# Pair attention kernel: the six pair adds that GpSimd makes per block, written in six other forms

## The chip, the cores and the metric

The kernel runs on one core of one Trainium2 chip. Its metric is the device time of one execution in microseconds (us), of which lower is better. A core has a TensorE for matmuls (PE in the profile, its weight loads PEld), a VectorE (DVE), a ScalarE (ACT), a GpSimd (POOL) and a SyncE (SP) that issues most DMAs. Each engine works through its own instructions in the order of the program, and waits on semaphores where it needs another engine's result.

## The reference

The reference is a network of two layers on an input of 4 sequences of 1024 tokens with 256 channels. Each layer has a layer norm with a modulation, an attention part, another modulated layer norm and a feed-forward part. Layer 0 is a recurrence over time followed by a mixture of eight experts. Layer 1, which the change belongs to, is a pair attention followed by a dense feed-forward net of hidden width 1024 (w1, w2, h1, h2, w3). Cut to what matters, its attention is:

```
q = einsum('bnc,ac->bna', X, Wq)          # 64 channels a
k = einsum('bnc,ac->bna', X, Wk)
Vy = einsum('bnc,dc->bnd', X, Wy_w) + Wy_b
e = relu(rho(q[:, :, None, :] + k[:, None, :, :]))
scores = einsum('bija,a->bij', e, Wphi)
ex = exp(scores - max(scores, axis=-1))
denom = sum(ex, axis=-1)
part1 = einsum('bij,bjc->bic', ex, Vy)
Ew = einsum('bij,bija->bia', ex, e)
part2 = einsum('bia,ca->bic', Ew, We_w) + We_b * denom
out = (part1 + part2) / (denom + 1e-9)
```

Here rho(x) is sqrt(relu(x) + 1e-8) - sqrt(relu(-x) + 1e-8). For every query i, key j and channel a the sum q + k is formed, clipped at zero, and its root taken. These are 4 x 1024 x 1024 x 64 values, and they set the work of this layer.

## The kernel before, in words

The first part of the kernel (to about 1088 us in the profile) computes layer 0 and the keys, queries and values of the first sequence. The rest is the function `pair_attention`, which computes the pair attention of layer 1, with its feed-forward net and the remainder of layer 0 woven in.

`pair_attention` works on N = 128 blocks of 32 queries each, 32 blocks for each of the 4 sequences. A block (class `Block`) has 16 tiles of 128 partitions x 1024 keys. A tile's partitions are 8 channels by 16 queries; its number i (0 to 15) says which of 8 channel groups and which half of the queries it holds. Two tiles make a pair p (0 to 7; i = 2p + h), which lies in one buffer of the ring "s" of RING = 14 buffers of 128 x 2 x 1024 floats. A buffer passes through these steps:

- The add: relu(key + query), where the keys kB[i % 8] are a 128 x 1024 tile in SBUF and the query is one number per partition, `self.query(i)`. Which engine makes it depends on i. In all blocks but the first, the six tiles of ADD_ON_POOL = (1, 3, 5, 9, 11, 13) are made by GpSimd in `begin` (line 1396), the five of RELU_ON_SCALAR = (2, 6, 8, 12, 14) by ScalarE in `pair` (line 1418), and the other five (0, 4, 7, 10, 15) by VectorE in `adds` (line 1407). The first block has none on GpSimd, so that GpSimd makes 127 x 6 = 762 adds.
- The root: ScalarE takes the square root of the whole pair in place (line 1419, 128 x 2048).
- The scores: TensorE multiplies the roots by the weights of their channels and adds them up in the block's PSUM tile "sc" (line 1423, 16 matmuls for a pair).
- When the block's 8 pairs are in, `top` (line 1433), `exps` (line 1442) and `spread` (line 1449) take the largest score, the exponentials, and spread these over the partitions into the PSUM tile "xb".
- `weigh` (line 1469): VectorE multiplies each of the 16 tiles by xb in place and sums along the keys into a column of "ew". After the second tile of a pair its ring buffer is free again.

The order on each engine is the order in which the Python code issues the instructions. The loop at the end of `pair_attention` goes over the blocks and over p. At each step it issues `weigh` for pair p of the present block and `adds` for the pair that is next to be finished, then (at p = 5 and 6) `top`, `exps` and `spread` of the next block, then a share of other work (`work`, which draws on the generators `finish` and `dense`), and then `begin` and `make` up to 14 pairs ahead. `begin` for a pair runs LEAD = 2 pairs ahead of `make`, which issues the rest of the add, the root and the scores. So GpSimd's adds run 2 pairs ahead of the root that needs them, and up to 14 pairs ahead of the `weigh` that frees their buffer.

`finish` ends four blocks at a time: it multiplies by values and weights, divides, and GpSimd adds the result to the residual (line 1544, "xr"). `dense` is the feed-forward net for 256 tokens (lines 1260 to 1362), whose last step is also an add on GpSimd (line 1362, "res"). In layer 0 GpSimd makes the products "kv" (line 745), products "rk" (line 437), the sums "xi" (line 414) and others, all of them tensor-by-tensor instructions.

Of the kernel before, what the change touches and what calls it, by code (L numbers as in the profile page):

```python
# [9 lines left out]
ALU = mybir.AluOpType  # L10
# [4 lines left out]
P = 128  # L15
B, T, C = 4, 1024, 256
# [19 lines left out]
FIRST_ON_SCALAR = 6  # L36
ADD_ON_POOL = (1, 3, 5, 9, 11, 13)
LEAD = 2

CONSTS = {"ident": P, "tri": P, "ones": P, "avg": P, "center": P, "heads": P, "gather": P, "rank": NE, "same": P, "pick": 4 * P, "part": 4, "query": 16, "row0": P}  # L40
CH_MX, CH_MW, CH_MK, CH_MV, CH_MR, CH_MG, CH_TD, CH_U, CH_LW, CH_LB = range(10)
# [3 lines left out]
def block_kernel(ctx: ExitStack, tc: tile.TileContext, a, out):  # L45
# [26 lines left out]
    nc.gpsimd.memset(seen, 0.0)  # L72
    first_layer(tc, a, link, cols, seen, ident, eps)
    pair_attention(tc, a, link, out, cols, seen, ident, eps)


# [762 lines left out]
def pair_attention(tc, a, link, out, cols_of, seen, ident, eps):  # L839
# [10 lines left out]
    nc = tc.nc  # L850
# [4 lines left out]
    with tc.tile_pool(name="at_k", bufs=1) as pk, tc.tile_pool(name="at_w", bufs=1) as wp, tc.tile_pool(  # L855
# [14 lines left out]
        kB, qtab, kds, vds = {0: {}}, {0: link["qt"][0]}, {0: link["kd"]}, {0: link["vd"]}  # L870
# [17 lines left out]
        for i in range(2):  # L888
            t = wp.tile([P, 4, P], F32, tag=f"ewt{i}", name=f"ewt{i}")
            nc.gpsimd.memset(t, 0.0)  # L890
            ewt.append(t)
            t = wp.tile([P, 4, 64], F32, tag=f"ew{i}", name=f"ew{i}")
# [485 lines left out]
        class Block:  # L1378
# [9 lines left out]
            def query(self, i):  # L1388
                return qtab[self.b][:, 2 * (self.n % NB) + i // 8, i % 8 : i % 8 + 1]

            def begin(self, p):
                self.s[p] = ring.tile([P, 2, T], F32, tag="s", name="s")
                for h in range(2):
                    i = 2 * p + h
                    if self.n and i in ADD_ON_POOL:
                        nc.gpsimd.tensor_scalar(  # L1396
                            self.s[p][:, h, :], kB[self.b][i % 8], self.query(i), 0.0, ALU.add, ALU.max
                        )

            def adds(self, p):  # L1400
                if p in self.added:
# [190 lines left out]

        for _ in range(LEAD):
            begin()
        for _ in range(8):
            begin()
            make()
# [3 lines left out]
        while begun < ahead[0]:  # L1601
            begin()
            make()
# [134 lines left out]
```

## Time and profile before

| What | Value |
|---|---|
| Two runs | 4984.17 us and 4977.72 us, median 4980.94 us |
| Span of the profiled execution, first to last instruction | 4972.7 us |
| GpSimd's adds of line 1396 | 762, from 1088.9 us to 4789.1 us, 2879.2 us busy |
| VectorE's adds of line 1407 | 645, 595.3 us busy |
| ScalarE's relus of line 1418 | 641, 728.9 us busy |
| ScalarE's roots of line 1419 | 1024, 2028.2 us busy |
| VectorE's weighing, line 1469 | 2048, 2419.0 us busy |

The record of the profiled execution has its span and no time of its own. The median of the two runs is 4980.94 - 4972.7 = 8.2 us above that span. A row of the profile's groups gives the line, the engine, the operation, output and inputs by the program's names, shapes and count, and after the bar the busy time in us, the mean duration of one in ns, the time that the engine sat idle just before these instructions, and what ended most of this idle time. Busy shares of several engines add up to more than the span, since they work side by side.

### The profile page before, as it was taken

How to read it: one execution, taken by the hardware profiler on the slowest of the kernel's cores; microseconds unless marked ns; L12 is line 12 of the kernel's file. 1: busy time of each engine (PE TensorE's matmuls, PEld its weight loads, DVE VectorE, ACT ScalarE, POOL GpSimd, SP SyncE). 2: the span in 40 equal slices, each digit the busy share in tenths (PEclk: the TensorE clock that was granted, in tenths of full speed). 3: DMA queues.
4: the chain of work that ended last, by engine and by line, in shares of the span. 5: the costliest groups of instructions: out<-in, count | busy, mean ns of one | idle time of the engine just before them, and what ended most of it. 6: DMA issues, size and time to landing. Idle time of an engine off the chain costs nothing.

```text
span 4972.7 us, 75609 instructions
## 1 busy us (share of the span) xinstructions
PE 4289.7 (86%) x28714; PEld 2423.9 (49%) x28714; DVE 4175.6 (84%) x7255; ACT 3688.3 (74%) x3436; POOL 3397.2 (68%) x1231
## 2 busy tenths in 40 slices
PE   6899999886879788988887988889798889888888
PEld 1233333332346455545554655545455555455557
DVE  5899999868998888898887888888888888888871
ACT  2333333238898898899998998999888989999961
POOL 3544444336887787888786887887777878887840
PEclk8799999887999899989997999999899999999999
DMA  4333333440022222312112332212132322112223
GB/s 139 94 117 116 108 110 111 131 141 19 23 65 85 74 90 68 125 56 79 64 62 81 108 108 83 71 58 86 48 119 75 110 70 86 60 69 76 73 83 113
DMA packets 255947, 429.42 MB, mean 86 GB/s; under 512 B 71784, under 2 KB 142624, under 8 KB 255328
## 3 DMA queue, kind: packets, MB, share of 16 engines
q1 hardware_dynamic: 252512, 422.09, 26.2%
q8 instruction: 227, 3.72, 0.3%
q10 hardware_dynamic: 2880, 1.98, 0.1%
q14 instruction: 136, 1.11, 0.1%
q0 software_dynamic: 192, 0.52, 0.0%
HBM read 400.32 MB, written 40.93 MB: 89 GB/s over the span
## 4 chain that ended last, share of the span: by engine, by line
PE 50%; DVE 20%; ACT 20%; issue 7%; DMA 1%; SPq 1%; POOL 1%; DVEq 0%; ACTq 0%; POOLq 0%
PE ff_ps L1330 14%; PE sc L1423 10%; ACT s L1419 9%; DVE s L1469 9%; PE e_ps L620 7%; ACT s L1418 4%; DVE s L1407 3%; PE xb L1449 3%; PE out_ps L1351 2%; PE o L1520 2%; PE proj_ps L425 2%; ACT L1419 2%; DVE state L813 1%; PE mix_ps L405 1%; ACT L1372 1%
## 5 line engine op out<-in xcount | busy, mean ns | idle before, releaser
L1396 POOL TENSOR_SCALAR s<-kB,qt 128x1024 f32<-128x1024 f32 x762 | 2879.2, 3792 | 603.5 <-DVE ew L1469 476.2
L1469 DVE CUSTOM_DVE_ANT_0 s<-s,xb 128x1024 f32<-128x1024 f32 x2048 | 2419.0, 1211 | 38.4 <-PE xb L1449 36.8
L1419 ACT ACTIVATE s<-s,eps 128x2048 f32<-128x2048 f32 x1024 | 2028.2, 2000 | 84.0 <-DVE s L1407 38.5
L1423 PE MATMUL sc<-s,wsel 128*32 128x256 f32 x16384 | 1199.1, 417 | 399.4 <-ACT s L1419 397.0
L1330 PE MATMUL ff_ps<-wide,fw 128*128 128x256 f32 x4096 | 1005.3, 395 | 29.4 <-ACT wide L1372 25.8
L1423 PEld LDWEIGHTS sc<-s,wsel 128*32 128x32 f32 x16384 | 456.8, 116 | 1002.7 <-ACT s L1419 593.6
L1330 PEld LDWEIGHTS ff_ps<-wide,fw 128*128 128x128 f32 x4096 | 765.4, 194 | 237.5 <-issue 99.4
L1418 ACT ACTIVATE s<-kB,qt 128x1024 f32<-128x1024 f32 x641 | 728.9, 1137 | 18.7 <-DVE acc L603 18.0
L1407 DVE TENSOR_SCALAR s<-kB,qt 128x1024 f32<-128x1024 f32 x645 | 595.3, 924 | 0.3 <-issue 0.3
L745 POOL TENSOR_TENSOR kv<-vb,out_k 128x512 f32<-128x512 f32 x256 | 324.5, 1276 | 236.9 <-DVE state L813 157.3
L620 PE MATMUL e_ps<-wd,hid 128*128 128x512 f32 x896 | 414.7, 609 | 7.4 <-DVE acc L603 4.8
L1449 PE MATMUL xb<-ex,pick 64*128 64x256 f32 x2048 | 324.3, 440 | 56.2 <-ACT ex L1442 56.2
L813 DVE TENSOR_TENSOR_SCAN state<-dec,carry,kv 128x512 f32<-128x512 f32 x256 | 326.1, 1274 | 22.6 <-ACT dec L800 16.8
L1449 PEld LDWEIGHTS xb<-ex,pick 64*128 64x128 f32 x2048 | 195.4, 206 | 193.8 <-ACT ex L1442 96.1
L620 PEld LDWEIGHTS e_ps<-wd,hid 128*128 128x128 f32 x896 | 169.9, 195 | 231.3 <-issue 217.4
L1260 PE MATMUL ff_ps<-wide,fw 128*128 128x256 f32 x1024 | 266.2, 409 | 6.1 <-ACT wide L944 5.8
L805 ACT COPY carry<-state 128x1 f32<-128x1 f32 x255 | 47.9, 188 | 297.9 <-DVE state L813 297.5
L1260 PEld LDWEIGHTS ff_ps<-wide,fw 128*128 128x128 f32 x1024 | 197.6, 202 | 64.8 <-issue 25.6
L1314 DVE TENSOR_TENSOR wide<-ff_ps,ffn_s 128x512 f32<-128x512 f32 x128 | 87.9, 687 | 166.9 <-PE ff_ps L1330 166.9
L1433 DVE TENSOR_REDUCE sc<-sc 128x1 f32<-128x256 f32 x128 | 54.9, 429 | 204.5 <-PE sc L1423 204.3
L1442 ACT ACTIVATE ex<-sc,neg 128x256 f32<-128x256 f32 x128 | 60.7, 474 | 199.1 <-DVE neg L1440 198.3
L815 DVE TENSOR_TENSOR pr<-state,rec 128x512 f32<-128x512 f32 x256 | 176.0, 688 | 37.8 <-ACT state L811 10.5
(253 smaller groups left out, 3965.8 us busy)
## 6 DMA issues: line engine op xcount, KB each, us to landing
fw<-in_ffw_dram SPq DMA_DIRECT2D x354, 512.0 KB
vb<-vd SPq DMA_DIRECT2D x1024, 64.0 KB
lent<-vd SPq DMA_DIRECT2D x64, 514.0 KB
wd<-in_w_down_dram SPq DMA_DIRECT2D x28, 1024.0 KB
kB<-kd SPq DMA_DIRECT2D x32, 512.0 KB
lent<-in_We_dram SPq DMA_DIRECT2D x32, 512.0 KB
kd<-nd SPq DMA_DIRECT2D x24, 512.0 KB
vd<-out_v SPq DMA_DIRECT2D x8, 512.0 KB
```

The source lines that it names most:

```text
L620: nc.tensor.matmul(ps, hid[:, k, t * P : (t + 1) * P], wd[:, k, :], start=k == 0, stop=k == HID // P - 1)
L745: nc.gpsimd.tensor_mul(kv, vb[:, g % 2, :], ready[u]["k"][:, n // HN, :])
L813: nc.vector.tensor_tensor_scan(s[:, 1 : U + 1], dec, kv, c, ALU.mult, ALU.add)
L1260: nc.tensor.matmul(ps[:, h, :], w[:, k, o : o + P], hT[:, k, :], start=k == 0, stop=k == 1)
L1330: nc.tensor.matmul(ps[:, h, :], w[:, k * P : (k + 1) * P], of[:, k, :], start=k == 0, stop=k == 7)
L1396: nc.gpsimd.tensor_scalar(self.s[p][:, h, :], kB[self.b][i % 8], self.query(i), 0.0, ALU.add, ALU.max)
L1407: nc.vector.tensor_scalar(self.s[p][:, h, :], kB[self.b][i % 8], self.query(i), 0.0, ALU.add, ALU.max)
L1418: nc.scalar.activation(t[:, h, :], kB[self.b][i % 8], AF.Relu, bias=self.query(i))
L1419: nc.scalar.activation(t, t, AF.Sqrt, bias=eps_rho)
L1423: nc.tensor.matmul(self.sc[32 * j : 32 * j + 32, 0:256], wsel[:, g, 16 * (1 - s) : 16 * (1 - s) + 32], t[:, h, 256 * j : 256 * (j + 1)], s ...
L1449: nc.tensor.matmul(xb[:, 256 * j : 256 * (j + 1)], pick[q, j % 2, s, :], self.ex[q, :], start=True, stop=True)
L1469: nc.vector.tensor_tensor_reduce(t[:, h, :], t[:, h, :], self.xb[s], 1.0, 0.0, ALU.mult, ALU.add, ew[:, self.n % 4, col : col + 1])
```

## The change

`begin` no longer issues one `tensor_scalar` with add and max for each of the six tiles. It calls a new method, `pool_add`, which writes each tile number in its own form. Tile 13 keeps the one instruction. The other five have two instructions each, the second of which works in place on the tile t that the first has written. All instructions go over 128 x 1024 floats.

| Tile | First instruction | Second instruction, in place |
|---|---|---|
| 13 | (k + query) max 0 | none |
| 3 | (k * 1) + query | (t min FLT_MAX) max 0 |
| 5 | (k + query) * 1 | t max 0 |
| 9 | tensor by tensor: k + query, the query's column read 1024 times | (t max 0) min FLT_MAX |
| 11 | k + query | (t max 0) + 0 |
| 1 | (k * 1) + query | (t max 0) * 1 |

The result is the same in each form. In all there are 11 instructions per block in place of 6, that is 127 x 11 = 1397 in place of 762.

```diff
+FLT_MAX = 3.4028234e38
...
+            def pool_add(self, i, t, k):
+                q = self.query(i)
+                if i == 13:
+                    nc.gpsimd.tensor_scalar(t, k, q, 0.0, ALU.add, ALU.max)
+                elif i == 3:
+                    nc.gpsimd.tensor_scalar(t, k, 1.0, q, ALU.mult, ALU.add)
+                    nc.gpsimd.tensor_scalar(t, t, FLT_MAX, 0.0, ALU.min, ALU.max)
+                elif i == 5:
+                    nc.gpsimd.tensor_scalar(t, k, q, 1.0, ALU.add, ALU.mult)
+                    nc.gpsimd.tensor_scalar_max(t, t, 0.0)
+                elif i == 9:
+                    nc.gpsimd.tensor_tensor(t, k, q.to_broadcast([P, T]), ALU.add)
+                    nc.gpsimd.tensor_scalar(t, t, 0.0, FLT_MAX, ALU.max, ALU.min)
+                elif i == 11:
+                    nc.gpsimd.tensor_scalar_add(t, k, q)
+                    nc.gpsimd.tensor_scalar(t, t, 0.0, 0.0, ALU.max, ALU.add)
+                else:
+                    nc.gpsimd.tensor_scalar(t, k, 1.0, q, ALU.mult, ALU.add)
+                    nc.gpsimd.tensor_scalar(t, t, 0.0, 1.0, ALU.max, ALU.mult)
+
             def begin(self, p):
                 self.s[p] = ring.tile([P, 2, T], F32, tag="s", name="s")
                 for h in range(2):
                     i = 2 * p + h
                     if self.n and i in ADD_ON_POOL:
-                        nc.gpsimd.tensor_scalar(
-                            self.s[p][:, h, :], kB[self.b][i % 8], self.query(i), 0.0, ALU.add, ALU.max
-                        )
+                        self.pool_add(i, self.s[p][:, h, :], kB[self.b][i % 8])
```

## The prediction

> **What bounds the kernel now.** I read the page's busy shares first, then the chain of work that ended last, then the groups; after these the answer for GpSimd's add line, the groups of GpSimd alone, and the busy times by window.
>
> ```profile
> span 4972.7 us, 75609 instructions
> ...
> PE 4289.7 (86%) x28714; PEld 2423.9 (49%) x28714; DVE 4175.6 (84%) x7255; ACT 3688.3 (74%) x3436; POOL 3397.2 (68%) x1231
> ...
> PE 50%; DVE 20%; ACT 20%; issue 7%; DMA 1%; SPq 1%; POOL 1%; DVEq 0%; ACTq 0%; POOLq 0%
> ...
> L1396 POOL TENSOR_SCALAR s<-kB,qt 128x1024 f32<-128x1024 f32 x762 | 2879.2, 3792 | 603.5 <-DVE ew L1469 476.2
> ```
>
> No engine fills the span, and the chain passes from TensorE to VectorE to ScalarE; GpSimd has 1% of it. By the pair stage alone, from 1300 to 4785 us, the engines stand much closer:
>
> ```profile
> 1300.00:4785.00 3485.00, 3008.21 (x24135) 1836.53 (x24136) 3050.34 (x5427) 3157.26 (x2367) 2773.91 (x776) 0.91 0.23 78
> ```
>
> The columns are the stretch, its length, then the busy time of PE, PEld, DVE, ACT and POOL, the granted clock (0.91), the DMA share and GB/s. ScalarE is busy for 91%, VectorE for 88%, TensorE for 86%, GpSimd for 80%. So GpSimd is off the path but only 711 us of 3485 away from filling the stage. The next question is who waits for whom at its adds.
>
> ```profile
> L1396 POOL TENSOR_SCALAR s<-kB,qt x762: 3689/3700/4664, 1088.9 to 4785.0; 128x1024 f32<-128x1024 f32 x191
> its engine sat idle before it (us, times) until:
>   DVE ew L1469: 476.2, 207
> ...
> who waited for it (us, times):
>   POOL xr L1544: 21.1, 11
>   ACT s L1419: 1.2, 1
>   PEld sc L1423: 0.2, 1
> ```
>
> GpSimd waits for VectorE's weighing to free a ring buffer; almost nobody waits for GpSimd. A cheaper add on GpSimd is therefore worth next to nothing by this route, while a dearer one costs nothing until the slack is used up, and from there all of it.
>
> **The price of the forms.** The only `tensor_scalar` of GpSimd in this trace is add with max: 3.70 us at the median and 3.79 in the mean. Back to back it is the same: these are three in 11.05 us, 3.68 each, after 1.87 us of idle time.
>
> ```profile
> 3003.42 11.05 POOL L1396 TENSOR_SCALAR s<-kB,qt 128x1024 f32<-128x1024 f32 x3 [1.87 <-DVE ew L1469]
> ```
>
> The other rows of GpSimd that help:
>
> ```profile
> L745 POOL TENSOR_TENSOR kv<-vb,out_k 128x512 f32<-128x512 f32 x256 | 324.5, 1276 | 236.9 <-DVE state L813 157.3 <-DMA vb<-vd 74.7 <-DMA wd<-in_w_down_dram 3.0
> L437 POOL TENSOR_TENSOR rk<-out_r,out_k 128x1024 f32<-128x1024 f32 x8 | 18.8, 2348 | 0.8 <-ACT out_r L430 0.8
> L890 POOL MEMSET ewt<- 128x512 f32 x2 | 1.0, 524 | 13.0 <-PE yp L776 13.0
> L893 POOL MEMSET ew<- 128x256 f32 x2 | 0.6, 311 | 0.0
> ```
>
> A memset grows by (524 - 311) / 256 = 0.83 ns per element, so 1024 elements would take 0.95 us, 0.10 of it fixed. A product of two tensors of 128x1024 takes 2.35 us. One tensor with two operations takes 3.70 us, more than two tensors with one operation: the cost of a `tensor_scalar` here is not in reading, it is in the operations.
>
> - Tile 13 keeps its instruction, 3.79 us.
> - Seven new instructions have two operations in other pairs (tiles 3 and 1 both of theirs, tile 5 its first, tiles 9 and 11 their second). Bounds: 0.95 us (memset) and 4.66 us (the longest add with max). The nearest row by far is the same instruction on the same shape, and I take its 3.79: 7 x 3.79 = 26.53 us.
> - Two have one operation (tile 5's max, tile 11's add). Bounds: 0.95 and 3.79 us. If the two operations of the known row share 3.70 - 0.10 = 3.60 us evenly, one takes 1.80 + 0.10 = 1.90 us, and with the 0.09 by which the known row's mean lies above its median 1.99. I take this, since it lies below the 2.35 of one operation that has to read two tensors: 2 x 1.99 = 3.98 us.
> - Tile 9's add of two operands: 2.35 us from the product's row. That its second operand repeats one column is shown nowhere; bounds 0.95 and 3.79.
> - The in-place second instruction follows its first on the same engine. Any wait between the two is bounded by 0 and by the 0.30 us that GpSimd's DMA of line 610 sat idle after the sum of line 608 that it sends, at most 5 x 0.30 = 1.5 us per block; I take 0, as the adds in the row above run back to back.
>
> Per block: 3.79 + 26.53 + 3.98 + 2.35 = 36.65 us, against 6 x 3.79 = 22.75 before.
>
> **From GpSimd's block to the time.** When GpSimd is the bound, the time is what stands before its first add, its queue, and what follows its last. Its first add starts at 1088.9 us. Its other instructions up to its last add take 47 us (148.4 busy from 1088.9 to 1300 and 2773.9 to 4785, less the adds). Of the 63 us that it sits idle in the first 211 us, where the rest of layer 0 is still running, I keep about half, 30. From the end of its last add at 4789.1 to the end of the span there are 184 us, in which two blocks are weighed and the last feed-forward group runs; that part is on other engines and keeps its length. Sum: 1089 + 47 + 30 + 184 = 1350, plus 127 blocks. With 22.75 us this floor is 1350 + 2889 = 4239, well under 4972.7; it reaches the span at (4972.7 - 1350) / 127 = 28.5 us per block, where the ten new instructions would have (28.5 - 3.79) / 10 = 2.47 us each. With 36.65 it is 1350 + 4655 = 6005 us. The median lies 8 us above the profiled span, so the forecast is 6013, rounded to **6010 us**.
>
> Behind GpSimd's late tile stands ScalarE's root of that pair (line 1419); behind this on ScalarE's queue are the next relus, the exponentials and the feed-forward activations, and TensorE's scores wait for the root. The ring does not take up the delay: 14 buffers hold 6 pairs more than a block, which smooths one late block, not 127. Nor do the residual adds (lines 1544 and 1362) on GpSimd's queue gain new waits: their inputs come from steps some 14 pairs older than the adds ahead of them.
>
> VectorE's own adds (line 1407) run beside GpSimd's: 739 ns at the least, 751 at the median, 924 in the mean, 2137 at the most. More instructions on GpSimd may stretch them. Bounds: all of the excess over the least goes, 645 x 0.185 = 119 us less, or each costs the most, 645 x 1.213 = 782 us more. In the forecast VectorE has at least 1000 us of idle time more than now, which covers either; I take 0.
>
> **Two rules against the rows.** The Trainium skill's page "GPSIMD Engine Reference", section 4.1 Engine selection, says of GpSimd's elementwise work that "1-input is roughly line-rate", which by its clock and width would be about 0.85 us for 1024 elements. The row of add with max, one input, says 3.70. By the rule the block would have 3.79 + 9 x 0.85 + 2.35 = 13.8 us and the change would be free, at 4981; I keep to the row. The page "SBUF — State Buffer", section Who interferes with whom, says that VectorE in a 2-port mode and GpSimd block each other for a whole instruction. VectorE's adds, 0.75 us at the median beside GpSimd's 3.70, do not show waits of that length.
>
> **The rivals.**
>
> - The forms are cheap and nothing changes (4980 us). The mechanism is a special path on GpSimd for other pairs of operations than add with max; it decides from a mean of 2.47 us for the ten new instructions. For it speaks the memset at 0.83 ns per element, which shows that the engine can go through elements four times as fast as in the add; against it that the only `tensor_scalar` seen goes at 3.6. Chance 0.20.
> - The same, and VectorE's adds also get their 119 us back with nearly all of it on the path: 4981 - 119 = 4862 us, 2.4% less. VectorE has but 20% of the chain. Chance 0.04.
> - Only max and min are dear. Then the three pairs of times and plus and the single add take 1.99 us, and the four pairs with max or min, the single max and tile 13 take 3.79: 6 x 3.79 + 4 x 1.99 + 2.35 = 33.05 us, 1350 + 4197 + 8 = 5555 us. Nothing in the profile parts the price of add from that of max. With it goes the case that the forms are cheap but VectorE's adds pay for it: 782 us less its 435 us of idle time in the stage, about 5330. Chance for 5080 to 5740 together 0.20.
> - One operation costs as much as two: 10 x 3.79 + 2.35 = 40.25 us, 1350 + 5112 + 8 = 6470 us, and with 0.30 us of wait for each second instruction 6660. Chance for over 6270: 0.18.
>
> **How the numbers follow.** The forecast's own case, 34.5 to 38.7 us per block or 5740 to 6270 us, has 0.38. A measurement of this kernel tells about 2%, 100 us, from no change. Faster by more has 0.04, within it 0.20, and slower by more 0.38 + 0.20 + 0.18 = 0.76. The range of 8 in 10 has to take in the unchanged case and the case of one price for all: 4960 to 6500 us, which leaves out the 0.04, a few in 100 just below it, and somewhat under half of the last rival.
>
> **What the profile after would show.** Right: 127 instructions for each of eleven forms, add with max near 3.79, the other pairs near that, the single ones near 2 and the two-operand add near 2.35; GpSimd busy at some 127 x 36.65 + 520 = 5170 us; its wait for VectorE's weighing down from 476.2 us to under 60; ScalarE's root waiting for GpSimd for several hundred us where it now waits 1.2; GpSimd with most of the chain. Wrong: a mean of the ten under 2.47 us, with the wait for the weighing still in the hundreds. The step most likely to fail is the price of the seven pairs: each 0.5 us on them moves the time by 7 x 0.5 x 127 = 445 us.

## The result, and the profile after

The changed kernel takes 5040.13 us (median of 5035.30 and 5044.96) against 4980.94: 1.0122 of before, with an interval of 1.0092 to 1.0152. It is slower by 59 us; the forecast was 6010, and a range of 4960 to 6500. The forecast loss was 1029 us and the real one 59, so the size is wrong by far.

These are lines of the page of the changed kernel: the span, the busy times, GpSimd's busy tenths in 40 slices, and the chain that ended last by engine.

```profile
span 5033.5 us, 76219 instructions
...
PE 4310.1 (86%) x28714; PEld 2433.2 (48%) x28714; DVE 4219.3 (84%) x7255; ACT 3694.1 (73%) x3436; POOL 4010.0 (80%) x1866
...
POOL 3544444347999899999998999999888999999950
...
PE 42%; DVE 19%; ACT 17%; POOL 11%; issue 8%; DMA 2%; SPq 1%; ACTq 0%; POOLq 0%; DVEq 0%
```

GpSimd's busy time grew by 613 us, not by the 1770 that the forecast had (5170 less 3397), and it now shows nines in most slices of the pair stage and 11% of the chain. Here are the groups of GpSimd alone, in the order of their cost. Lines 1395 to 1410 are the eleven new forms in the order of the diff: 1395 is tile 13, 1397 and 1398 tile 3, 1400 and 1401 tile 5, 1403 and 1404 tile 9, 1406 and 1407 tile 11, 1409 and 1410 tile 1.

```profile
L1404 POOL TENSOR_SCALAR s<-s 128x1024 f32<-128x1024 f32 x127 | 500.5, 3941 | 11.8
L1395 POOL TENSOR_SCALAR s<-kB,qt 128x1024 f32<-128x1024 f32 x127 | 493.7, 3887 | 0.8 <-PE sc L1442 0.8
L1410 POOL TENSOR_SCALAR s<-s 128x1024 f32<-128x1024 f32 x127 | 478.5, 3768 | 11.0
L1407 POOL TENSOR_SCALAR s<-s 128x1024 f32<-128x1024 f32 x127 | 472.3, 3719 | 10.5
L1406 POOL TENSOR_SCALAR s<-kB,qt 128x1024 f32<-128x1024 f32 x127 | 364.8, 2873 | 71.9 <-DVE ew L1488 58.7 <-DVE ln_rs L931 7.6 <-ACT s L1437 3.8
L1401 POOL TENSOR_SCALAR s<-s 128x1024 f32<-128x1024 f32 x127 | 361.1, 2844 | 11.2
...
L1403 POOL TENSOR_TENSOR s<-kB,qt 128x1024 f32<-128x1024 f32 x127 | 252.9, 1991 | 5.7 <-DVE neg L1459 5.7
L1409 POOL TENSOR_SCALAR s<-kB,qt 128x1024 f32<-128x1024 f32 x127 | 149.9, 1180 | 13.9
L1397 POOL TENSOR_SCALAR s<-kB,qt 128x1024 f32<-128x1024 f32 x127 | 145.3, 1144 | 13.4 <-DVE ew L1488 7.8 <-DVE before L129 5.2 <-PE sc L1442 0.3
L1400 POOL TENSOR_SCALAR s<-kB,qt 128x1024 f32<-128x1024 f32 x127 | 141.7, 1116 | 30.2 <-DVE ew L1488 17.6 <-DVE ln_rs L931 0.9 <-ACT s L1438 0.4
L1398 POOL TENSOR_SCALAR s<-s 128x1024 f32<-128x1024 f32 x127 | 135.4, 1067 | 11.1
```

The number to read is the mean of one, after the busy time. There are two kinds of pair of operations. Times then plus (1.14 and 1.18 us), plus then times (1.12) and min then max (1.07) are cheap. Plus then max (3.89), max then min (3.94), max then plus (3.72) and max then times (3.77) cost three times as much. A single operation (2.87 and 2.84) costs more than a cheap pair of two. The eleven means add up to 27.53 us per block, just under the prediction's break-even of 28.5. GpSimd's wait for the ring (releaser DVE ew), 476.2 us before, is 58.7 + 17.6 + 7.8 = 84 us here.

Two more groups show who pays: ScalarE's root and VectorE's own adds. The first line is the root before the change; VectorE's adds took 924 ns in the mean then.

```profile
L1419 ACT ACTIVATE s<-s,eps 128x2048 f32<-128x2048 f32 x1024 | 2028.2, 2000 | 84.0 <-DVE s L1407 38.5 <-POOL s L1396 1.2 <-ACT s L1418 0.4
```

And these are both after it:

```profile
L1438 ACT ACTIVATE s<-s,eps 128x2048 f32<-128x2048 f32 x1024 | 2034.2, 2001 | 163.3 <-POOL s L1407 62.4
...
L1426 DVE TENSOR_SCALAR s<-kB,qt 128x1024 f32<-128x1024 f32 x645 | 640.0, 993 | 0.3 <-issue 0.3
```

Roots now wait for GpSimd: 62.4 us after tile 11's second pass, and with those after tiles 13 and 1 103 us (1.2 before). And VectorE's adds take 993 ns in the mean, 924 before, 45 us in all. So there are two theories for the 59 us. **Theory A**: GpSimd is late. **Theory B**: GpSimd's new instructions get in the way of VectorE's adds (called contention below). There is a third suspect, for which no run was made: the granted clock of TensorE is 0.904 here and 0.910 before, and TensorE is busy 20 us longer with the same matmuls. The loss is spread over the stage: VectorE's first weighing of block 32 begins 17 us later than before, of block 64 30 us, of block 96 49 us.

### The profile page after: what moved, and what is told of

It reads as the page before. It is cut to its first block, busy times and chain, and to the rows that moved or that the text cites. A ratio compares the mean times of both kernels' runs of the same rounds, so it can differ in the third digit from the quotient of the medians.

```text
span 5033.5 us, 76219 instructions
## 1 busy us (share of the span) xinstructions
PE 4310.1 (86%) x28714; PEld 2433.2 (48%) x28714; DVE 4219.3 (84%) x7255; ACT 3694.1 (73%) x3436; POOL 4010.0 (80%) x1866
## 3 DMA queue, kind: packets, MB, share of 16 engines
q8 instruction: 227, 3.72, 0.3%
## 4 chain that ended last, share of the span: by engine, by line
PE 42%; DVE 19%; ACT 17%; POOL 11%; issue 8%; DMA 2%; SPq 1%; ACTq 0%; POOLq 0%; DVEq 0%
PE ff_ps L1331 10%; DVE s L1488 8%; ACT s L1438 8%; PE sc L1442 8%; PE e_ps L621 7%; ACT s L1437 3%; DVE s L1426 2%; POOL s L1395 2%; PE out_ps L1352 2%; PE xb L1468 2%; POOL s L1410 2%; PE proj_ps L426 2%; POOL s L1407 1%; POOL s L1406 1%; DVE state L814 1%
## 5 line engine op out<-in xcount | busy, mean ns | idle before, releaser
L1438 ACT ACTIVATE s<-s,eps 128x2048 f32<-128x2048 f32 x1024 | 2034.2, 2001 | 163.3 <-POOL s L1407 62.4
L1331 PEld LDWEIGHTS ff_ps<-wide,fw 128*128 128x128 f32 x4096 | 763.6, 194 | 234.8 <-issue 97.1
L1426 DVE TENSOR_SCALAR s<-kB,qt 128x1024 f32<-128x1024 f32 x645 | 640.0, 993 | 0.3 <-issue 0.3
L1404 POOL TENSOR_SCALAR s<-s 128x1024 f32<-128x1024 f32 x127 | 500.5, 3941 | 11.8
L1395 POOL TENSOR_SCALAR s<-kB,qt 128x1024 f32<-128x1024 f32 x127 | 493.7, 3887 | 0.8 <-PE sc L1442 0.8
L1410 POOL TENSOR_SCALAR s<-s 128x1024 f32<-128x1024 f32 x127 | 478.5, 3768 | 11.0
L1407 POOL TENSOR_SCALAR s<-s 128x1024 f32<-128x1024 f32 x127 | 472.3, 3719 | 10.5
L1406 POOL TENSOR_SCALAR s<-kB,qt 128x1024 f32<-128x1024 f32 x127 | 364.8, 2873 | 71.9 <-DVE ew L1488 58.7
L1401 POOL TENSOR_SCALAR s<-s 128x1024 f32<-128x1024 f32 x127 | 361.1, 2844 | 11.2
```

The lines of the kernel that those rows point to most:

```text
L1331: nc.tensor.matmul(ps[:, h, :], w[:, k * P : (k + 1) * P], of[:, k, :], start=k == 0, stop=k == 7)
L1395: nc.gpsimd.tensor_scalar(t, k, q, 0.0, ALU.add, ALU.max)
L1404: nc.gpsimd.tensor_scalar(t, t, 0.0, FLT_MAX, ALU.max, ALU.min)
L1407: nc.gpsimd.tensor_scalar(t, t, 0.0, 0.0, ALU.max, ALU.add)
L1410: nc.gpsimd.tensor_scalar(t, t, 0.0, 1.0, ALU.max, ALU.mult)
L1426: nc.vector.tensor_scalar(self.s[p][:, h, :], kB[self.b][i % 8], self.query(i), 0.0, ALU.add, ALU.max)
```

## The experiments

All of them change only the forms of the adds, or which tiles GpSimd has; the number in brackets after a ratio is its interval.

**The fast form on all six tiles.** Tile 3's form, two cheap pairs, for every tile of GpSimd:

```diff
-nc.gpsimd.tensor_scalar(t, k, q, 0.0, ALU.add, ALU.max)
+nc.gpsimd.tensor_scalar(t, k, 1.0, q, ALU.mult, ALU.add)
+nc.gpsimd.tensor_scalar(t, t, FLT_MAX, 0.0, ALU.min, ALU.max)
```

> All six tiles in the form of tile 3: times one plus query, then min and max. By the prices measured in the changed kernel (1.14 and 1.07 us) GpSimd's adds take 6 x 2.21 = 13.3 us per block, half of before. Theory A (GpSimd is late): the 59 us of the change come from roots that wait for GpSimd; here nothing waits for it, and the time is that of before, 4960 to 5000 us, with ScalarE's root waiting under 5 us for GpSimd. Theory B (contention): the 59 us come from VectorE's adds, which met more and faster passes of GpSimd (924 to 993 ns); here there are 12 such passes per block, so VectorE's adds stay at 990 ns or more and the time stays at 5020 us or above.

4978.35 us, 0.9992 of before (0.9982 to 1.0001). The groups of GpSimd and VectorE's adds in this run:

```profile
L1398 POOL TENSOR_SCALAR s<-kB,qt 128x1024 f32<-128x1024 f32 x762 | 858.6, 1127 | 1575.4 <-DVE ew L1470 1340.6 <-PE sc L1424 71.2 <-DVE ln_rs L931 26.1
L1399 POOL TENSOR_SCALAR s<-s 128x1024 f32<-128x1024 f32 x762 | 845.3, 1109 | 66.8
```

```profile
L1408 DVE TENSOR_SCALAR s<-kB,qt 128x1024 f32<-128x1024 f32 x645 | 587.2, 911 | 0.3 <-issue 0.3
```

GpSimd's adds fall from 2879 to 1704 us and it waits 1341 us for the ring; the time does not move. This shows what the waits of before said: a cheaper add on GpSimd alone is worth nothing. VectorE's adds fell too, to 911 ns, so this run speaks for A only so far as B's own expectation (990 ns) did not come about.

**The same sum from add with max.** The old form on all six, and two passes that change no value:

```diff
+if i == 11:
+    nc.gpsimd.tensor_scalar(t, t, 0.0, 0.0, ALU.max, ALU.add)
+elif i == 13:
+    nc.gpsimd.tensor_scalar(t, t, FLT_MAX, 0.0, ALU.min, ALU.max)
```

> The kernel of before, with two passes more that change no value: max with 0 plus 0 on tile 11 (3.72 us) and min, max on tile 13 (1.07 us). GpSimd's adds then take 22.75 + 4.79 = 27.54 us per block, the same sum as the changed kernel's 27.53, in 8 instructions in place of 11. Theory A: the sum sets the time, so 5020 to 5060 us, with roots waiting for GpSimd over 100 us. Theory B: the passes that are fast on GpSimd set it, of which there is one per block here against four there, so 4980 to 5000 us.

5087.72 us, 1.0207 (1.0192 to 1.0223): more than either theory gave. VectorE's adds and ScalarE's root:

```profile
L1411 DVE TENSOR_SCALAR s<-kB,qt 128x1024 f32<-128x1024 f32 x645 | 608.7, 945 | 0.3 <-issue 0.3
```

```profile
L1423 ACT ACTIVATE s<-s,eps 128x2048 f32<-128x2048 f32 x1024 | 2031.1, 2000 | 233.0 <-POOL s L1402 117.7 <-POOL s L1400 48.2 <-DVE s L1411 26.5
```

VectorE's adds are only 13 us longer in all than before, and the time is 106 us longer, with 169 us of roots waiting for GpSimd. So there is a loss below the break-even with hardly any stretch of VectorE's adds, and the sum alone does not set its size. TensorE is busy 43 us longer here, at a clock of 0.897.

**Far above the break-even.** All six tiles in tile 11's form:

```diff
-nc.gpsimd.tensor_scalar(t, k, q, 0.0, ALU.add, ALU.max)
+nc.gpsimd.tensor_scalar_add(t, k, q)
+nc.gpsimd.tensor_scalar(t, t, 0.0, 0.0, ALU.max, ALU.add)
```

> All six tiles in the form of tile 11: plus query alone (2.87 us), then max with 0 plus 0 (3.72 us), 6 x 6.59 = 39.5 us per block. If the prediction's floor is right (1350 us plus 127 blocks plus 8), 1350 + 5022 + 8 = 6380 us, between 6330 and 6430, with GpSimd busy for over 95% of the pair stage. If engines lose more to each other than the floor has, over 6430.

6400.69 us, as expected within 21 us. GpSimd's tenths and the root:

```profile
POOL 4444434999999999999999999999999999999980
```

```profile
L1420 ACT ACTIVATE s<-s,eps 128x2048 f32<-128x2048 f32 x1024 | 2049.0, 2002 | 1677.6 <-POOL s L1399 1656.6 <-DVE s L1408 5.6
```

Here GpSimd fills the stage and ScalarE's root waits 1657 us for it. The prediction's floor holds where GpSimd is clearly the bound.

**Other pairs.** One pair on each tile, beside cheap ones. The question is the price of each; the lines are shortened.

```diff
+tensor_scalar(t, t, 0.0, 0.0, ALU.max, ALU.max)         # tile 1, second
+tensor_scalar(t, t, 1.0, 0.0, ALU.mult, ALU.max)        # tile 3, second
+tensor_scalar(t, t, 0.0, 0.0, ALU.add, ALU.max)         # tile 5, second
+tensor_scalar(t, k, q, 0.0, ALU.add, ALU.add)           # tile 9, first
+tensor_scalar(t, k, q, FLT_MAX, ALU.add, ALU.min)       # tile 11, first
+tensor_scalar(t, k, -FLT_MAX, q, ALU.max, ALU.add)      # tile 13, first
```

> Prices of other pairs, each on one tile, values unchanged: max with max (tile 1), times with max (3), plus with max where both are constants (5), as second instructions; plus with plus (9), plus with min (11), max with plus query (13), as first ones. If the price hangs on whether max or min is in the pair, all but plus with plus are dear (near 3.7 us). If a few pairs have a path of their own and min, max is one of them, the same is expected here, and plus with plus near 1.1 us. If the column operand is what makes plus with max dear, the one with constants takes near 1.1 us. The time is not the question; by the sum it is near that of before.

The groups of GpSimd; the order is max with plus query (1414), plus with min (1411), plus with max of constants (1406), max with max (1400), plus with plus (1408), times with max (1403).

```profile
L1414 POOL TENSOR_SCALAR s<-kB,qt 128x1024 f32<-128x1024 f32 x127 | 503.2, 3962 | 3.6 <-PE sc L1440 2.5 <-PE k_ps L1000 1.0
L1411 POOL TENSOR_SCALAR s<-kB,qt 128x1024 f32<-128x1024 f32 x127 | 499.1, 3930 | 30.4 <-DVE ew L1486 13.6 <-PE xb L1466 7.6 <-ACT ex L1459 3.8
L1406 POOL TENSOR_SCALAR s<-s 128x1024 f32<-128x1024 f32 x127 | 490.9, 3866 | 11.1
L1400 POOL TENSOR_SCALAR s<-s 128x1024 f32<-128x1024 f32 x127 | 479.3, 3774 | 11.0
L1408 POOL TENSOR_SCALAR s<-kB,qt 128x1024 f32<-128x1024 f32 x127 | 472.9, 3724 | 0.1
L1403 POOL TENSOR_SCALAR s<-s 128x1024 f32<-128x1024 f32 x127 | 467.2, 3679 | 11.1
```

All six are dear, plus with plus among them, which has neither max nor min, and plus with max of two constants too. So what makes a pair dear is neither max nor the column operand alone. All expectations but the second (a few pairs with a path of their own) fall, and this one missed plus with plus. The constants were always 0, 1 and the largest float or its negative; others were not tried. All of GpSimd's passes here come to 29.65 us per block, and the one execution of this kernel took 5216 us, where the floor gives 1350 + 3766 + 8 = 5124.

**The place of the dear passes.** The same two passes, on tiles 1 and 9:

```diff
-if i == 11:
+if i == 1:
...
-elif i == 13:
+elif i == 9:
```

> The run with add with max on all six tiles and two passes more, moved: max with 0 plus 0 now on tile 1 and min, max on tile 9, in place of tiles 11 and 13. Instructions and their sum (27.5 us per block) are the same. Theory P (place): it took 5088 us, and not the changed kernel's 5040, because its dear passes stood at the end of the block's adds, where the exponentials wait for the last roots; moved to the front it takes 5000 to 5050 us, and roots wait for GpSimd under 100 us in all. Theory S (the sum and the slow passes alone): 5075 to 5095 us again.

5019.50 us, 1.0082 (1.0065 to 1.0098). The same instructions in other places cost 68 us less, as theory P of its expectation said; but roots still wait 104 us for GpSimd (55.5 and 48.7 at its two lines), against its "under 100". A second test of place takes the changed kernel and exchanges the forms of tiles 3 and 11:

```diff
-elif i == 3:
+elif i == 11:
...
-elif i == 11:
+elif i == 3:
```

> The changed kernel with the forms of tiles 3 and 11 exchanged: the same eleven instructions per block, 27.5 us, but the tile of 6.6 us is now near the front of the block and that of 2.2 us near its end. Theory P (dear tiles at the end of the block delay its exponentials): 5000 to 5025 us, roots waiting for GpSimd under 60 us. If only the sum counts: 5035 to 5045 us as the changed kernel.

5065.93 us, 1.0174 (1.0160 to 1.0188): 26 us worse than the changed kernel, where theory P had it better.

```profile
L1438 ACT ACTIVATE s<-s,eps 128x2048 f32<-128x2048 f32 x1024 | 2028.7, 2000 | 270.0 <-POOL s L1407 184.0 <-DVE s L1426 35.9 <-POOL s L1410 4.4
```

Roots wait 184 us for the dear tile, which is now tile 3. That dear tiles hurt at the end of a block and not at its front has fallen. The third test spreads the sum evenly:

```diff
+if i in (5, 11):
+    nc.gpsimd.tensor_scalar_add(t, k, q)
+    nc.gpsimd.tensor_scalar(t, t, FLT_MAX, 0.0, ALU.min, ALU.max)
+else:
+    nc.gpsimd.tensor_scalar(t, k, 1.0, q, ALU.mult, ALU.add)
+    nc.gpsimd.tensor_scalar(t, t, 0.0, 0.0, ALU.max, ALU.add)
```

> The same sum spread evenly: tiles 5 and 11 by a single add and then min, max (3.94 us), the other four by times one plus query and then max with 0 plus 0 (4.87 us), 27.4 us per block. If bunched dear tiles make GpSimd late: roots wait for GpSimd under 60 us and the time is 4990 to 5020 us. If the sum alone does: 5035 us or more.

5055.29 us, 1.0149 (1.0134 to 1.0164), with 155 us of roots waiting for GpSimd. Bunching isn't it either. The runs with 27.5 to 27.9 us per block, as measured, lie between 5020 and 5088 us; what in the placing decides stays open. The last two runs do clear the third suspect as far as lateness goes: TensorE is busy 4304 and 4283 us in them, 4290 before, so roots that wait for GpSimd come with a loss of 74 to 87 us where TensorE takes at most 14 us more.

**One form of the changed kernel mended.** Tile 9 gets min before max:

```diff
-nc.gpsimd.tensor_scalar(t, t, 0.0, FLT_MAX, ALU.max, ALU.min)
+nc.gpsimd.tensor_scalar(t, t, FLT_MAX, 0.0, ALU.min, ALU.max)
```

> The changed kernel with one form mended: tile 9's second instruction has min before max (1.07 us) in place of max before min (3.94). GpSimd's adds take 27.53 - 2.87 = 24.66 us per block, under the 28.5 of the break-even by 3.8. Theory A (GpSimd's lateness): nearly all of the 59 us go, 4975 to 5000 us. Theory B (contention with VectorE's adds): one fast pass more, VectorE's adds stay at 990 ns or above, 5030 us or more.

5016.52 us, 1.0076 (1.0061 to 1.0091), between the theories. The first pass of tile 11 on GpSimd, then VectorE's adds:

```profile
L1406 POOL TENSOR_SCALAR s<-kB,qt 128x1024 f32<-128x1024 f32 x127 | 362.3, 2853 | 366.4 <-DVE ew L1488 322.8 <-DVE ln_rs L931 19.0 <-ACT ex L1461 6.9
```

```profile
L1426 DVE TENSOR_SCALAR s<-kB,qt 128x1024 f32<-128x1024 f32 x645 | 636.2, 987 | 0.3 <-issue 0.3
```

GpSimd waits 323 us for the ring again, so it has slack, and roots wait 37 us for it in place of 103. Yet 40 us of loss (5016.52 against 4976.93 of the kernel before, run beside it) remain, with VectorE's adds at 987 ns and TensorE busy 27 us longer than before. So theory A doesn't have it all.

**Contention by itself.** The tensor-by-tensor add on all six tiles, with a cheap second pass:

```diff
+nc.gpsimd.tensor_tensor(t, k, q.to_broadcast([P, T]), ALU.add)
+nc.gpsimd.tensor_scalar(t, t, FLT_MAX, 0.0, ALU.min, ALU.max)
```

> All six tiles with the tensor-by-tensor add of tile 9 (1.99 us) and then min, max (1.07 us): 6 x 3.06 = 18.4 us per block, so GpSimd is never late. In the traces so far a VectorE add that begins while this tensor-by-tensor add runs takes 1.32 us, against 0.75 with GpSimd idle. Theory B (contention costs by itself): VectorE's adds rise to 1000 ns or more in the mean and the time rises with them, by half of their rise or more: from 645 x 0.08 = 52 us, 25 to 60 us over before, 5005 to 5040. Theory A (lateness alone): VectorE's adds may stretch, but the time stays within 10 us of before, since no root waits for GpSimd.

5072.45 us, 1.0184 (1.0170 to 1.0197). GpSimd's add, VectorE's adds and ScalarE's root:

```profile
L1398 POOL TENSOR_TENSOR s<-kB,qt 128x1024 f32<-128x1024 f32 x762 | 1445.0, 1896 | 1109.2 <-DVE ew L1470 952.5 <-ACT s L1420 35.3 <-DVE ln_rs L931 33.1
```

```profile
L1408 DVE TENSOR_SCALAR s<-kB,qt 128x1024 f32<-128x1024 f32 x645 | 754.8, 1171 | 0.3 <-issue 0.3
```

```profile
L1420 ACT ACTIVATE s<-s,eps 128x2048 f32<-128x2048 f32 x1024 | 2030.3, 2000 | 105.3 <-DVE s L1408 60.5 <-POOL s L1399 0.5
```

GpSimd is far from late (18.4 us per block, roots wait 0.5 us for it) and VectorE's adds grew by 160 us; the time grew by 93. So GpSimd's instructions can cost time without being late. That the cost goes through VectorE's adds fits the chain, of which VectorE has 29% here and 20% before; but TensorE is also busy 78 us longer (4367.5, at a clock of 0.891), and no run tells whether this is part of the cause or follows from the waits. To see how much of this loss the changed kernel has, its tensor-by-tensor add was exchanged at the same sum:

```diff
-nc.gpsimd.tensor_tensor(t, k, q.to_broadcast([P, T]), ALU.add)
-nc.gpsimd.tensor_scalar(t, t, 0.0, FLT_MAX, ALU.max, ALU.min)
+nc.gpsimd.tensor_scalar_add(t, k, q)
+nc.gpsimd.tensor_scalar_max(t, t, 0.0)
```

> The changed kernel with tile 9's tensor-by-tensor add and max, min (5.93 us) exchanged for a single add and a single max (2.87 + 2.84 = 5.71 us): 27.3 us per block, no tensor-by-tensor add left. If the meeting of that add with VectorE's adds carries a large part of the 59 us: VectorE's adds fall to 950 to 970 ns and the time to 5005 to 5025 us. If lateness carries it: VectorE's adds may fall, but the time stays at 5030 to 5045 us.

5033.42 us, 1.0107 (1.0092 to 1.0122), which can't be told from the changed kernel's 1.0122 (1.0092 to 1.0152).

```profile
L1426 DVE TENSOR_SCALAR s<-kB,qt 128x1024 f32<-128x1024 f32 x645 | 605.8, 940 | 0.3 <-issue 0.3
```

```profile
L1438 ACT ACTIVATE s<-s,eps 128x2048 f32<-128x2048 f32 x1024 | 2035.2, 2001 | 160.4 <-POOL s L1407 66.6 <-POOL s L1395 31.1 <-DVE s L1426 16.0
```

34 of the 45 us of VectorE's stretch are gone and the roots still wait for GpSimd as before (104 us in all); the loss stays at 53 us. So most of the loss stays without most of the stretch, as the second case of the expectation has it. With lateness mostly taken away and the stretch left, 40 us stay; with the stretch mostly taken away, 53 stay. The two do not add up to the 59, and how the loss divides between them stays open.

**Spending the fast form.** GpSimd has room for more tiles at 2.2 us each. The lists changed are ADD_ON_POOL and RELU_ON_SCALAR:

```diff
-ADD_ON_POOL = (1, 3, 5, 9, 11, 13)
+ADD_ON_POOL = (1, 3, 5, 7, 9, 11, 13, 15)                 # two of VectorE's
+ADD_ON_POOL = (1, 3, 5, 6, 9, 11, 12, 13)                 # two of ScalarE's
+ADD_ON_POOL = (1, 3, 5, 6, 7, 9, 11, 12, 13, 15)          # two of each
+ADD_ON_POOL = (1, 2, 3, 5, 6, 8, 9, 11, 12, 13)           # four of ScalarE's
+ADD_ON_POOL = (0, 1, 3, 4, 5, 7, 9, 10, 11, 13, 15)       # all of VectorE's
+ADD_ON_POOL = (0, 1, 3, 4, 5, 6, 7, 9, 10, 11, 13, 15)    # and one of ScalarE's
```

Two of VectorE's:

> All tiles of GpSimd in the fast form (2.24 us a tile), and tiles 7 and 15 moved from VectorE to GpSimd: 8 tiles, 17.9 us per block. VectorE is relieved of 2 x 0.91 = 1.8 us of 29.1 per block. If VectorE carries its share of the stage (20% of the chain), 1 to 3% less, 4830 to 4940 us. Rival: ScalarE (91% of the stage) and TensorE set it alone, 4960 to 4990 us.

Two of ScalarE's:

> The fast form on 8 tiles, the two more (6 and 12) taken from ScalarE alone; VectorE keeps its five. The run that took two from VectorE gained nothing, the one that took two from each gained 1.0%. If ScalarE is what the stage hangs on: 4900 to 4940 us, as the run with 10 tiles. If VectorE and ScalarE bound it by turns, so that both must be relieved: 4960 to 4985.

Two of each ("before that" is the run with two of VectorE's):

> As before that, and tiles 6 and 12 moved from ScalarE to GpSimd as well: 10 tiles, 22.4 us per block, which is what GpSimd had before with 6. ScalarE is relieved of 2 x 1.14 = 2.3 us per block. If the stage hangs on ScalarE and VectorE together, 4 to 7% less than before, 4630 to 4790 us. Rival: TensorE, whose work per block stays at 25.1 us, sets it: no more than 1% below the run with 8 tiles.

Four of ScalarE's:

> The fast form on 10 tiles, all four more (2, 6, 8 and 12) taken from ScalarE, which keeps tile 14: 4 x 1.14 = 4.6 us per block less on ScalarE. If ScalarE is the bound: 4830 to 4900 us. If VectorE and TensorE take over after the first two tiles: 4900 to 4950 us.

All of VectorE's:

> The fast form on 11 tiles, among them all five that VectorE had after the first block; ScalarE keeps its five. 11 x 2.27 = 25 us per block on GpSimd, and VectorE makes no add that could meet it. If contention ate the gain of the run that took two tiles from VectorE: 4880 to 4940 us. If ScalarE is the bound whatever VectorE does: 4960 to 4990 us.

All of VectorE's and one of ScalarE's:

> As that, with tile 6 taken from ScalarE as well: 12 tiles, 12 x 2.25 = 27 us per block, near GpSimd's break-even of 28.5, no add on VectorE. If relief of ScalarE and the end of contention add up: 4850 to 4920 us. If GpSimd is late again at 27 us per block: 4980 us or more, with roots waiting for it over 100 us.

| Tiles moved to GpSimd | Time, us | Ratio to before (interval) | VectorE's add, mean | Roots waiting for GpSimd |
|---|---|---|---|---|
| 2 of VectorE's | 4985.75 | 1.0013 (1.0003 to 1.0024) | 998 ns | 1 us |
| 2 of ScalarE's | 4948.48 | 0.9937 (0.9923 to 0.9951) | 966 ns | 3 us |
| 2 of each | 4926.55 | 0.9895 (0.9879 to 0.9912) | 1053 ns | 6 us |
| 4 of ScalarE's | 4948.55 | 0.9939 (0.9925 to 0.9953) | 1025 ns | 167 us |
| all 5 of VectorE's | 4935.22 | 0.9910 (0.9893 to 0.9926) | none after block 0 | 4 us |
| 5 of VectorE's, 1 of ScalarE's | 4979.95 | 1.0003 (0.9993 to 1.0012) | none after block 0 | 180 us |

For the first row its rival came, for the fourth the second case, for the fifth the first. The second row lies between its two cases, and the last, with roots waiting 180 us, is late as its second case said. The best, two of each, is 1.0% faster than the kernel before, not the 4 to 7% expected; its rival there, TensorE, had at most 1% below the first row, and 1.2% came. The chain of that run by engine:

```profile
PE 58%; DVE 22%; ACT 11%; issue 5%; DMA 1%; POOL 1%; SPq 1%; ACTq 0%; DVEq 0%; POOLq 0%
```

TensorE has 58%, 50% before: with ScalarE relieved it takes over most. Relief of VectorE alone gained only where all its adds went; beside that of ScalarE two tiles of it gained another 22 us. These are GpSimd's two passes in the run of the last row:

```profile
L1398 POOL TENSOR_SCALAR s<-kB,qt 128x1024 f32<-128x1024 f32 x1524 | 1709.3, 1122 | 195.3 <-DVE ew L1470 30.8 <-DVE neg L1441 10.7 <-DVE ln_rs L931 8.6
L1399 POOL TENSOR_SCALAR s<-s 128x1024 f32<-128x1024 f32 x1524 | 1586.1, 1041 | 133.6
```

So GpSimd is late again at about 26 us per block ((1709.3 + 1586.1) / 127), well below 28.5. In the fourth row roots wait 167 us for it at only 23 us ((1494.0 + 1442.0) / 127), and the relief of ScalarE by two more tiles than in the second row gained nothing.

## Why the prediction was wrong

- **The bound and the waits** before the change were read rightly: GpSimd is off the path, and a cheaper add is worth nothing (the fast form: 0.9992).
- **"The nearest row by far is the same instruction on the same shape, and I take its 3.79: 7 x 3.79 = 26.53 us."** This step failed. The seven took 1.14 + 1.07 + 1.12 + 3.94 + 3.72 + 1.18 + 3.77 = 15.94 us. For three of them the row was right within 4%; for four it was three times too high, since the price hangs on the pair of operations. One price for all of an instruction's forms was assumed from one form, and the lower bound of 0.95 from the memset was the better guide for those four. The reading behind it, that the cost of a `tensor_scalar` "is in the operations", doesn't hold as a matter of their number: four passes of two operations took 1.07 to 1.18 us, and one of a single operation 2.84.
- **The single operations** were taken at 1.99 us and took 2.84 and 2.87: halving a pair's price failed. The tensor-by-tensor add was taken at 2.35 and took 1.99. The step between the two in-place passes was taken at 0 and shows 11 us of idle time in 127, 0.09 us each.
- **The sum** came to 27.53 us per block for 36.65, and this difference alone is 9.12 x 127 = 1158 us of the forecast. It took GpSimd from far above the break-even of 28.5 to just under it.
- **The floor** (1350 + 127 blocks) was right where GpSimd is clearly the bound: with 39.64 us per block it gives 6393 us, and 6401 were measured. But with 27.53 it gives 4854, less than before, and the kernel took 5040. That a dearer add "costs nothing until the slack is used up" is the second step that failed: the break-even at 28.5 was used as a sharp edge, and the runs show losses of 0.8 to 2.1% at 27.5 to 27.9 us, and a loss of 45 us against its neighbour at 26.
- **VectorE's adds, "I take 0"**, rested on idle time that a GpSimd-bound stage would give. That cover was gone, and the adds took 45 us more. In the run with six tensor-by-tensor adds 160 us of stretch came with 93 us of time. What the 45 us cost in the changed kernel isn't settled: with 34 of them gone the time is 7 us less, which is within the noise.
- **The rival "the forms are cheap and nothing changes"** had the right mechanism for four of ten forms and the mean (2.36 us against its 2.47), and the wrong end: just under the edge is not free. That 5040 lies inside the range is owed to this rival, for which the range was stretched down to 4960; the forecast's own case was 5740 to 6270. Of the two signs of being wrong only the first came in full, the mean of 2.36; the wait for the weighing fell to 84 us, since the adds had used up most of the slack.

The rule of the Trainium skill that was weighed, "1-input is roughly line-rate" ("GPSIMD Engine Reference", section 4.1 Engine selection), which the prediction estimated at 0.85 us, is near for the three cheap pairs (1.07 to 1.18 us) and wrong by a factor of three or more for the other pairs and for single operations.

## What to carry to other kernels

Price an instruction on GpSimd with the very pair of operations that it will have: here times-plus, plus-times and min-max (in that order) took about a third of what the eight other pairs that were tried did, and of the forms tried a relu after an add is cheapest as two instructions, 2.2 us in place of 3.8. Making an engine that is off the path faster is worth no gain by itself, and a dearer one begins to cost before its busy time reaches the period of the others. Here the period was 29.1 us per block (3700 us of adds over 127 blocks); 24 us with eleven tiles kept roots waiting 4 us, 26 us with twelve 180 us, and 23 us with ten, otherwise chosen, 167 us. So no share of slack can be named, and where the work stands counts too. Measure also what the other engines' instructions take beside the new form.

## What was not expected of the hardware

- A VectorE add that begins while GpSimd runs a tensor-by-tensor add took 1.61 us in the mean of 297, and 0.75 in the mean of 307 with GpSimd idle (from the starts and ends in the trace of the run with six of them). Waiting for the end of a 1.90-us instruction from a random point would make 0.75 + 0.95 = 1.70, by estimate. Beside the dear passes of tile 11's form (2.9 and 3.7 us) the same add took 0.95 us in the mean of 631, where such a wait would make over 2. The rule of the Trainium skill's "SBUF — State Buffer" (section Who interferes with whom), that of GpSimd and VectorE in a 2-port mode one is blocked for the whole instruction of the other, would agree with the first of these and not with the second; no run here shows in which mode VectorE's adds went.
- The granted clock of TensorE was 0.824 over the run in which GpSimd was clearly the bound, against 0.910 before, and TensorE's busy time rose from 4290 to 4667 us with the same matmuls.
